# Transposing the first eight groups' input weights beside stage 0, and eight x tiles instead of ten

## The chip, the cores and the metric

The kernel runs on one NeuronCore of a Trainium2 chip. The metric is the device time of one execution in microseconds (us). PE is the tensor engine (PEld its weight loads), DVE the vector engine, ACT the scalar engine, POOL the GpSimd engine, SP the engine that here only issues transfers. SBUF is the on-chip memory, PSUM the accumulators that PE writes.

## The reference, cut to what matters

Two layers, each added to its input. B = 64 batches, C = 128 channels, L = 2048 steps.

```python
W = weights[condition]                       # [64, 128, 128], one of 16 matrices for each batch
x = x + einsum('bct,bcd->bdt', x, W)         # layer 0: a projection of the channels
K = 2 * einsum('hn,hnl->hl', Ct, exp(dtA * arange(L))).real     # 64 complex modes for each channel
y = irfft(rfft(x, 2L) * rfft(K, 2L))[..., :L] + x * D           # layer 1: causal convolution by channel
x = x + y * (arange(L) < length)             # masked by each batch's length
```

Everything is float32.

## The kernel before, in words

L is cut into two segments of 1024 steps (`SEGS`). The kernel has three parts.

**Stage 0** projects segment 0. For each of the 64 batches, `batch0(b)` calls `project`: eight matmuls (line 472) into a PSUM tile of the tag `y`, a copy back into the x tile on ACT or DVE (line 474), and a transfer of 0.5 MiB to a scratch array in DRAM (`scr`, line 477, issued by ACT). An x tile `xb` holds two batches, 1 MiB. `fetch` (line 442, issued by SP) loads it. `batch0(2n)` fetches tile `n + AHEAD`, with `AHEAD = 9` and ten tiles in the pool `big`, so that tile n + 10 needs the buffer of tile n. Beside the batches run the parameters of layer 1: first the setup on DVE and ACT, then, in the loop over `now` from 12 to 63, the tables `es` of 16 groups of channel pairs (steps `angles`, `sines`, `products`) and the first lags of the convolution kernel (`lags`, `keep_lags`, `store_lags`).

**The loop** `iteration(i)` goes over 64 pairs of segment and group: i = 0 to 31 are the 32 groups of four channels of segment 0, i = 32 to 63 those of segment 1. Iteration i prepares item i + 1 and finishes item i. On PE it holds: the transposes of the input weights of item i + 1 (`input_weights`, line 799, segment 0 alone, four transposes into a PSUM tile of the tag `tr`, copied by ACT at line 800 into `bt`), the transposes of x (`turn`, line 816, tag `tr`), the matmuls with the input weights (`inputs`, line 838), the direct part of the convolution (`inside`, line 883), the part from the states (`read`, line 891), and, in segment 0, the projection of segment 1 in pieces of 512 steps (`some`, line 467, tag `tr`): 12 pieces ahead of the loop, the other 116 in 28 iterations. The tag `tr` has two buffers. DVE does the recurrence (`scan`, line 853) and the masked result (line 913).

The input weights `bt` of a group are the same in both segments. In segment 0 they are transposed and stored to DRAM (`keep_weights`, line 805, 256 KiB, issued by SP); in segment 1 SP loads them back (line 792).

**The x tiles of the loop** come from the same pool `big`: `load(i + 3)` at line 778 for item i + 3 and, for the projection, `fetches` (line 442) of one `xb` tile in most iterations. SP takes its instructions strictly in order: in iteration i they are `load(i + 3)`, the fetch, four stores of item i - 1 (line 927), and the store of the weights of item i + 1. Each transfer that needs a buffer waits on SP until that buffer's last user is done.

**Semaphores of transfers.** The transfers issued by SP and ACT share eight completion semaphores, taken in turn in recorded order. A transfer is not issued until the one eight places ahead of it in that order has landed. ACT issues the `scr` stores, so ACT itself stands still in such a wait, with all that is queued behind it.

Of the kernel before, what the change touches and what calls it, by code (L numbers as in the profile page):

```python
# [42 lines left out]
F32 = mybir.dt.float32  # L46
# [6 lines left out]
P = 128  # L53
# [16 lines left out]
TP = 4  # L70
# [305 lines left out]
def cond_resid_ssm_kernel(  # L376
# [13 lines left out]
    nc = tc.nc  # L390
# [3 lines left out]
    N = a_imag.shape[1]  # L394
    NS = len(SEGS)
# [6 lines left out]
    GP = 8 // KK  # L402
# [3 lines left out]
    NE = Q + 1  # L406
# [6 lines left out]
    I8 = mybir.dt.uint8  # L413
    const = ctx.enter_context(tc.tile_pool(name="const", bufs=1))
    tab = ctx.enter_context(tc.tile_pool(name="tab", bufs=1))
    big = ctx.enter_context(tc.tile_pool(name="big", bufs=10))
    s0 = ctx.enter_context(tc.tile_pool(name="s0", bufs=4))
    dram = ctx.enter_context(tc.tile_pool(name="dram", bufs=1, space=DRAM))
    psp = ctx.enter_context(tc.tile_pool(name="psp", bufs=1, space=PSUM))

    scr = [dram.tile([P, C, HL], F32, tag=f"scr{s}", name=f"scr{s}") for s in range(NS)]
    kpad = dram.tile([C, KP], F32, tag="kpad", name="kpad")
    btd = dram.tile([NG, P, GP * 4 * N], F32, tag="btd", name="btd")
    carry = dram.tile([NP, P, 2, B], F32, tag="carry", name="carry")

    ci = const.tile([1, B], I32, tag="ci", name="ci")
    wres = const.tile([P, S, C], F32, tag="wres", name="wres")
    ident = const.tile([P, P], F32, tag="ident", name="ident")
# [3 lines left out]
    xbs, w1s = {}, {}  # L432
    BT = 2
    QB = SL // BK
    AHEAD = 9
    WAHEAD = 3

    def fetch(s, n):

        xbs[s, n] = big.tile([P, BT, SL], F32, tag="x", name=f"xb_{s}_{n}")  # L440
        src = x[n * BT : (n + 1) * BT, :, s * SL : (s + 1) * SL]
        nc.sync.dma_start(xbs[s, n], src.rearrange("b c t -> c b t"))
# [39 lines left out]
    def batch0(b, copy=nc.scalar.copy):  # L482
        if b % BT == 0 and b // BT + AHEAD < B // BT:
            fetch(0, b // BT + AHEAD)
        if b + WAHEAD < B:
            weigh(0, b + WAHEAD)
        project(0, b, 0, psp.tile([P, QB, BK], F32, tag="y", name=f"p0_0_{b}", bufs=2), QB, copy)

    V = nc.vector
    es = [tab.tile([P, TP, 2, NE], F32, tag=f"e{g}", name=f"e_{g}") for g in range(NT)]  # L490
# [4 lines left out]
    def exps(g):  # L495

        for i in range(TP):
            nc.scalar.activation(es[g][:, i, 0, :], steps, AF.Exp, scale=par_of(DRE, g, i))  # L498
# [11 lines left out]
    with tc.tile_pool(name="setup", bufs=1) as setup:  # L510
# [4 lines left out]
        par = _Parameters(nc, setup, psp, wk, ident, log_dt, c_in, log_a_real, a_imag)  # L515
        for n in range(AHEAD):
            fetch(0, n)
# [103 lines left out]
    def partial_angles(k):  # L621

        own = parts[:, :, 0:NL]
        by_l = some_l.unsqueeze(1).to_broadcast([P, NP, NL])

        def of(row, n):
            return gtab[:, row, :].unsqueeze(2).to_broadcast([P, NP, n])

        if k == 0:
            V.tensor_tensor(own, of(FHI, NL), by_l, ALU.mult)  # L630
        elif k == 1:
            V.tensor_scalar(whole, own, MAGIC, MAGIC, ALU.add, ALU.subtract)
        elif k == 2:
            V.tensor_tensor(own, own, whole, ALU.subtract)
        elif k == 3:
            V.tensor_tensor(whole, of(FLO, NL), by_l, ALU.mult)
        elif k == 4:
            V.tensor_tensor(own, own, whole, ALU.add)
        else:
            V.tensor_tensor(parts[:, :, 0:8], parts[:, :, 0:8], of(PHI, 8), ALU.add)  # L640
            V.tensor_tensor(parts[:, :, 24:25], parts[:, :, 24:25], of(PHI, 1), ALU.add)
            V.tensor_scalar(last, parts[:, :, 24:25], MAGIC, MAGIC, ALU.add, ALU.subtract)
            V.tensor_tensor(last, parts[:, :, 24:25], last, ALU.subtract)
# [48 lines left out]
    def store_lags(g):  # L692
# [3 lines left out]
        for c in range(2):  # L696
            r0 = g % 4 * 8 + c
            nc.gpsimd.dma_start(to[c], krow[r0 : r0 + 3 * 34 + 1 : 34, :])

    SPAN = 28  # L700
    pieces = [(s, b, q) for s in range(1, NS) for b in range(B) for q in range(QB)]
    FILL = 12
# [2 lines left out]
    def due(i):  # L705

        return min(len(pieces), FILL + (len(pieces) - FILL) * (i + 1) // SPAN)

# [7 lines left out]
    def fetches(n):  # L716

        nonlocal begun
        while begun < min(n + BT * QB, len(pieces)):
            fetch(pieces[begun][0], pieces[begun][1] // BT)  # L720
            begun += BT * QB
# [19 lines left out]
    for now in range(12, B):  # L741
        batch0(now, V.tensor_copy if now < 18 else nc.scalar.copy)
        if now < 20:

            by_row = d_in.rearrange("(d c h j) -> c d j h", j=8, c=2, d=2)
            with nc.allow_non_contiguous_dma(reason="128 gains, four times"):
                for i, r in ((i, r) for i in range(TP) for r in range(4) if (i * 4 + r) // 2 == now - 12):
                    nc.gpsimd.dma_start(dcol[i * NR + r : (i + 1) * NR : 4, :], by_row[r % 2, r // 2])
        if now == 21:
            V.tensor_scalar(dcol, dcol, 1.0, None, ALU.add)  # L750
        if now < FIRST:
            partial_angles(now - 12)
        if now < 18:
            exps(2 * now - 20)
            exps(2 * now - 19)
        for lag, step in STEPS.items():
            g, odd = divmod(now - FIRST - lag, 2)
            if not odd and 0 <= g < NT:
                step(g)
        if now == 60:  # L760
            fetches(FILL)
    assert not ts and not ks
# [5 lines left out]
    xs, us, ss, bts, tts, ys = {}, {}, {}, {}, {}, {}  # L768
# [3 lines left out]
    def seg(i):  # L772
        return divmod(i, NG)
# [11 lines left out]
        nc.gpsimd.dma_start(tts[i], bass.AP(row.tensor, row.offset, [[1, P], [KP, CG], [1, Q]]))  # L785

    def input_weights(i):

        s, g = seg(i)
        bts[i] = s1.tile([P, GP, 4, N], F32, tag="bt", name=f"bt_{i}")  # L790
        if s > 0:
            nc.sync.dma_start(bts[i].rearrange("p d k m -> p (d k m)"), btd[g])
            return
        pb = psp.tile([P, GP, 4, N], F32, tag="tr", name=f"pb_{i}", bufs=2)
        for d in range(GP):
            pair = g * GP + d
            for part in range(2):
                to = pb[:, d, part : 4 - part : 3 - 2 * part, :]
                nc.tensor.transpose(to, es[pair // TP][:, pair % TP, part, 1:NE], ident)  # L799
        nc.scalar.copy(bts[i], pb)  # L800

    def keep_weights(i):
        s, g = seg(i)
        if s == 0 and NS > 1:
            nc.sync.dma_start(btd[g], bts[i].rearrange("p d k m -> p (d k m)"))

    def at(s, d, f):
# [126 lines left out]
    def iteration(i):  # L934

        nxt = i + 1 < NI
        if i + 2 < NI and seg(i + 2)[0] > 0:
            input_weights(i + 2)
# [3 lines left out]
        if nxt:  # L942
            toeplitz(i + 1)
            if seg(i + 1)[0] == 0:
                input_weights(i + 1)
            states(i + 1)
# [13 lines left out]
        if nxt:  # L960
            inputs(i + 1, CG - 1)
            keep_weights(i + 1)
            scan(i + 1, 0, 2 if seg(i + 1)[0] == 0 else 1)
# [46 lines left out]
```

## Time and profile before

| what | value |
|---|---|
| median of 3 runs | 1116.4 us (1115.19 to 1116.72) |
| the profiled execution | 1110.19 us, span 1108.4 us |
| PE busy | 1054.6 us, 95% of the span |
| DVE, ACT, POOL busy | 821.4, 673.7, 222.6 us |
| granted PE clock, mean | 0.989 |
| moved by DMA | 313.31 MB |
| chain that ended last | PE 82%, DMA 12%, DVE 3%, ACT 2% |

The page cuts the span into 40 slices of 27.7 us; in its rows each digit is a busy share in tenths. The chain is followed back from the last instruction, at each step to what released it. The wait list gives who waited for whom, the total in us, the times and the longest. "DMA" as a row is the mean busy share of the 16 DMA engines.

### The profile page before, as it was taken

Reading aid. Unit: us, or ns where it says so; the run is one execution under the profiler, and the core shown is the slowest. Engines: PE = TensorE matmul, PEld = TensorE weight load, DVE = VectorE, ACT = ScalarE, POOL = GpSimd, SP = SyncE. Lnnn points to the kernel's source line nnn. Section 1 sums busy time; section 2 is a strip of 40 time slices with the busy share of each in tenths; the row PEclk is TensorE's granted clock in tenths of the full one; section 3 lists DMA queues with packets and bytes.
Section 4 is the critical chain, followed back from the end, with each engine's and each line's share of the span. In section 5 each row is a group of like instructions: output and inputs, shape, how many; then the busy total and the mean of one; then the engine's idle time right before and its main releaser. Section 6 shows DMA issues by size and latency. Waiting matters only on the chain.

```text
span 1108.4 us, 24477 instructions
## 1 busy us (share of the span) xinstructions
PE 1054.6 (95%) x8842; PEld 752.7 (68%) x8842; DVE 821.4 (74%) x2914; ACT 673.7 (61%) x1103; POOL 222.6 (20%) x386
## 2 busy tenths in 40 slices
PE   5678888999999999999999999999999999999996
PEld 2122223677777776776777778788888888888885
DVE  7587730667667766766766768888888888888886
ACT  3486665666666666667656666656665666566552
POOL 3152332021121112112121111212111111111120
PEclk9799999999999999999999999999999999999999
DMA  9999999999999999999999878688878887888754
GB/s 346 414 405 395 398 397 375 406 324 282 343 304 287 302 309 297 296 311 297 289 303 304 253 234 230 212 222 242 226 214 228 236 230 209 234 233 224 213 164 119
DMA packets 142731, 313.31 MB, mean 283 GB/s; under 512 B 12882, under 2 KB 13010, under 8 KB 142610
## 3 DMA queue, kind: packets, MB, share of 16 engines
q1 hardware_dynamic: 96528, 218.65, 62.6%
q10 hardware_dynamic: 35106, 67.64, 16.0%
q0 software_dynamic: 10976, 25.45, 8.7%
q8 instruction: 70, 1.15, 0.4%
q14 instruction: 51, 0.42, 0.1%
HBM read 164.76 MB, written 146.93 MB: 281 GB/s over the span
## 4 chain that ended last, share of the span: by engine, by line
PE 82%; DMA 12%; DVE 3%; ACT 2%; issue 1%; ACTq 0%; SPq 0%; DVEq 0%
PE y L891 20%; PE y L883 20%; PE v L838 19%; PE tr L816 10%; PE p L467 9%; DMA xb<-in_x_dram 6%; DMA scr<-xb 4%; PE p L472 2%; PE pb L799 2%; DMA x<-scr 1%; DVE s L853 1%; ACT xb L474 1%; DVE xb L474 0%; DVE x L913 0%; ACT e L498 0%
## 5 line engine op out<-in xcount | busy, mean ns | idle before, releaser
L853 DVE SCALAR_TENSOR_TENSOR s<-s,ptab 128x128 f32<-128x128 f32 x1792 | 535.9, 344 | 193.7 <-ACT s L843 193.7
L843 ACT ACTIVATE s<-v,ptab 64x512 f32<-64x512 f32 (+1 forms) x512 | 335.6, 655 | 51.3 <-PE v L838 35.1
L883 PEld LDWEIGHTS y<-tt,u 128*128 128x128 f32 x2048 | 263.5, 192 | 80.5 <-issue 67.0
L883 PE MATMUL y<-tt,u 128*128 128x128 f32 x2048 | 269.9, 275 | 0.1
L891 PEld LDWEIGHTS y<-e,s 64*128 64x128 f32 (+1 forms) x4096 | 219.0, 181 | 52.1 <-issue 26.6
L838 PE MATMUL v<-u,bt 128*128 128x512 f32 (+1 forms) x512 | 248.7, 567 | 0.3 <-ACT s L843 0.3
L817 ACT COPY u<-tr 128x512 f32<-128x512 f32 x252 | 148.1, 588 | 152.4 <-PE tr L816 125.7
L891 PE MATMUL y<-e,s 64*128 64x128 f32 (+1 forms) x4096 | 237.3, 276 | 1.4 <-DVE s L853 1.4
L474 ACT COPY xb<-p 128x512 f32<-128x512 f32 (+1 forms) x186 | 133.2, 717 | 80.8 <-PE p L467 54.1
L913 DVE COPY_PREDICATED x<-mask,y 128x1024 f32<-128x1024 uint8 x128 | 166.7, 1302 | 1.0 <-PE y L891 1.0
L472 PE MATMUL p<-xb,w 128*64 128x512 f32 x512 | 128.3, 639 | 37.2 <-issue 15.6
L816 PE MATMUL tr<-ident,x 128*128 128x128 f32 x1024 | 155.5, 274 | 1.7 <-DMA x<-scr 0.9
L816 PEld LDWEIGHTS tr<-ident,x 128*128 128x128 f32 x1024 | 121.1, 141 | 51.4 <-issue 44.9
L456 POOL COPY w<-wres 128x128 f32 x125 | 53.7, 430 | 426.7 <-PE p L467 315.6
L467 PE MATMUL p<-xb,w 128*128 128x512 f32 x256 | 129.6, 596 | 0.9 <-issue 0.6
L472 PEld LDWEIGHTS p<-xb,w 128*64 128x64 f32 x512 | 38.2, 144 | 112.1 <-issue 106.9
L838 PEld LDWEIGHTS v<-u,bt 128*128 128x128 f32 x512 | 79.5, 191 | 14.9 <-issue 13.4
L785 POOL DMA_DIRECT2D tt<-kpad x64 | 50.5, 789 | 194.7 <-DVE s L853 166.6
L863 DVE TENSOR_SCALAR s<-s 128x64 f32<-128x64 f32 x448 | 86.5, 193 | 0.0
L826 POOL DMA_DIRECT2D s<-carry x64 | 44.9, 706 | 127.1 <-PE y L891 118.4
L800 ACT COPY bt<-pb 128x512 f32<-128x512 f32 x32 | 18.7, 586 | 79.8 <-PE pb L799 75.6
L874 POOL DMA_DIRECT2D carry<-s x64 | 43.6, 722 | 100.9 <-DVE s L853 92.1
(194 smaller groups left out, 357.6 us busy)
## 6 DMA issues: line engine op xcount, KB each, us to landing
xb<-in_x_dram SPq DMA_DIRECT2D x64, 1024.0 KB, 9.5
scr<-xb ACTq DMA_DIRECT2D x128, 512.0 KB, 7.7
x<-scr SPq DMA_DIRECT2D x64, 1024.0 KB, 8.3
out_dram<-x SPq DMA_DIRECT2D x130, 256.0 KB, 3.7
out_dram<-x SPq DMA_DIRECT2D x62, 512.0 KB, 4.6
tt<-kpad POOLq DMA_DIRECT2D x64, 256.0 KB, 5.6
btd<-bt SPq DMA_DIRECT2D x32, 256.0 KB, 4.6
bt<-btd SPq DMA_DIRECT2D x32, 256.0 KB, 4.8
```

The lines of the kernel that those rows point to most:

```text
L467: nc.tensor.matmul(ps[:, k], w1s[s, b], own[:, cols[0]], start=True, stop=True)
L472: nc.tensor.matmul(ps[c, k], w1s[s, b][:, c], own[:, cols[h]], start=True, stop=True)
L474: copy(own[:, cols], ps.rearrange("p k t -> p (k t)"))
L816: nc.tensor.transpose(tr[:, k, :], xs[i][:, n, k * Q : (k + 1) * Q], ident)
L817: (nc.vector.tensor_copy if i == 0 else nc.scalar.copy)(u, tr)
L838: nc.tensor.matmul(v[:, 0:nv], w, us[i, n].rearrange("p k r -> p (k r)")[:, 0:nv], start=True, stop=True)
L843: nc.scalar.activation(own[:, 0:nv], v[lanes, 0:nv], AF.Copy, scale=amp)
L853: nc.vector.scalar_tensor_tensor(new, src, factor, own, ALU.mult, ALU.add)
L863: nc.vector.tensor_scalar(old[d][:, 2], old[d][:, 0], -1.0, None, ALU.mult)
L883: nc.tensor.matmul(y[:, k, :], u[:, k, :], tts[i][:, n, :], start=(k == 0), stop=False, skip_group_check=True)
L891: nc.tensor.matmul(ys[i, d][rows, c, k, :], ss[i][half[c], d, part, k, :, :].rearrange("p f b -> p (f b)")[:, rows], es[pair // TP][half[c ...
L913: nc.vector.copy_predicated(xs[i][:, 2 * d : 2 * d + 2, :].rearrange("r c (k t) -> r c k t", k=KK), keep_k.unsqueeze(1).to_broadcast([P, 2 ...
```

## The change

A tile `bres` of 8 groups' input weights (16 KiB of each partition) is added. In stage 0, at `now` = 37, 39, ..., 51, a new function transposes the weights of one of the groups 0 to 7 and DVE copies them into it. In the loop, the first eight groups of both segments use that tile; they are neither transposed there, nor stored, nor loaded back. The room comes from the pool `big`: eight tiles of 8 KiB instead of ten, and `AHEAD` is 7 instead of 9.

```diff
-    big = ctx.enter_context(tc.tile_pool(name="big", bufs=10))
+    big = ctx.enter_context(tc.tile_pool(name="big", bufs=8))
...
+    RG = 8
+    bres = const.tile([P, RG, GP, 4, N], F32, tag="bres", name="bres")
...
-    AHEAD = 9
+    AHEAD = 7
...
+    def weights_of(g, copy):
+
+        pb = psp.tile([P, GP, 4, N], F32, tag="tr", name=f"pb_{g}", bufs=2)
+        for d in range(GP):
+            pair = g * GP + d
+            for part in range(2):
+                to = pb[:, d, part : 4 - part : 3 - 2 * part, :]
+                nc.tensor.transpose(to, es[pair // TP][:, pair % TP, part, 1:NE], ident)
+        copy(bres[:, g] if g < RG else bts[g], pb)
...
+        g, even = divmod(now - 37, 2)
+        if not even and 0 <= g < RG:
+            weights_of(g, V.tensor_copy)
...
     def input_weights(i):
-
         s, g = seg(i)
+        if g < RG:
+            bts[i] = bres[:, g]
+            return
         bts[i] = s1.tile([P, GP, 4, N], F32, tag="bt", name=f"bt_{i}")
         if s > 0:
             nc.sync.dma_start(bts[i].rearrange("p d k m -> p (d k m)"), btd[g])
-            return
-        pb = psp.tile([P, GP, 4, N], F32, tag="tr", name=f"pb_{i}", bufs=2)
...
-        nc.scalar.copy(bts[i], pb)
+        else:
+            weights_of(g, nc.scalar.copy)
...
-        if s == 0 and NS > 1:
+        if s == 0 and g >= RG:
             nc.sync.dma_start(btd[g], bts[i].rearrange("p d k m -> p (d k m)"))
```

More of the change, by code (lines that the diff above doesn't have):

```diff
@@ L792, in input_weights @@
             nc.sync.dma_start(bts[i].rearrange("p d k m -> p (d k m)"), btd[g])
-            return
-        pb = psp.tile([P, GP, 4, N], F32, tag="tr", name=f"pb_{i}", bufs=2)
[L795 to L799, printed above, removed]
-        nc.scalar.copy(bts[i], pb)
+        else:
+            weights_of(g, nc.scalar.copy)
     def keep_weights(i):
         s, g = seg(i)
-        if s == 0 and NS > 1:
+        if s == 0 and g >= RG:
             nc.sync.dma_start(btd[g], bts[i].rearrange("p d k m -> p (d k m)"))
```

## The prediction

> **What bounds the kernel now.** I read the page's slices first, then the chain of waits in order of time, then two stretches of busy time, then the waits of SP's queue and ACT's timeline, last the landing times of single transfers. The slices:
>
> ```profile
> PE   5678888999999999999999999999999999999996
> DVE  7587730667667766766766768888888888888886
> DMA  9999999999999999999999878688878887888754
> ```
>
> The kernel has two limits in turn. In the first seven slices (stage 0) DMA is full and PE is not; from the eighth on PE is full. The busy time of four stretches says it in numbers (PE, PEld, DVE, ACT, POOL, then PE's clock, DMA share, GB/s):
>
> ```profile
> 54.60:78.60 24.00, 17.45 (x68) 5.13 (x65) 20.83 (x28) 21.02 (x55) 15.54 (x22) 0.93 1.04 407
> 80.90:162.50 81.60, 69.99 (x509) 23.17 (x500) 52.46 (x110) 51.55 (x77) 25.86 (x60) 0.98 1.03 396
> 315.00:656.00 341.00, 341.00 (x2735) 244.96 (x2732) 238.57 (x921) 217.47 (x358) 61.12 (x103) 1.00 0.93 293
> ```
>
> A share of 1.03 to 1.05 is the most this trace shows. From 54.6 to 78.6 DVE and ACT are nearly full as well; in segment 0 of the loop DMA, at 0.93, is close behind PE. The chain in segment 0, when no projection is left, with two starts of an iteration:
>
> ```profile
> 685.87 0.58 PE pb L799 x4
> 686.46 0.44 PE tr L816 x4
> ...
> 695.21 3.48 PE y L891 x64
> 698.69 0.59 PE tr L816 x4
> ```
>
> PE follows PE without a gap, so whatever leaves PE shortens the iteration. SP's queue, and ACT in front of a transfer:
>
> ```profile
> SPq L442 <- DMA scr<-xb: 144.0, 32, 7.2
> SPq L442 <- DMA out_dram<-x: 30.7, 21, 2.7
> 32.64 1.28 ACT L498 ACT_TABLE_LOAD   x1 [4.27 <-DMA scr<-xb]
> ```
>
> The first row: in stage 0 the fetches stand waiting for a store to land, that is, for a buffer. The third: ACT can be held by a transfer's semaphore, here for 4.27 us.
>
> **The change, part by part.** All sums are made against the profiled execution, 1110.19 us (span 1108.4 and 1.8 around it), and carried over to the median of 1116.4, which stands 6.2 higher.
>
> *Transposes leave the loop.* An iteration that starts with `pb` spends 0.58 + 0.44 us up to the end of the first `tr`, one without 0.59: 0.44 us saved a group (four matmuls of 0.11). Group 0's transposes run at 192.3, while PE waits for the first x tile (landed at 193.7): nothing saved. Groups 1 to 7: 7 x 0.44 = 3.05. At group 1 there is more:
>
> ```profile
> 201.67 0.89 PE y L883 x8
> 202.57 0.56 issue
> 203.12 1.10 PE p L467 x2
> ```
>
> The projection waits 0.56 for a `tr` buffer, and what ACT has just finished (202.44 to 203.02) is the copy of `bt`. With neither tile nor copy, the wait should go; what is late next is the recurrence's input on ACT, which is not on the chain there. Sum: -3.6 us (bounds -3.0 and -3.6). The eight ACT copies (0.59 each) and the eight stores and eight loads of 256 KiB cost nothing either way: ACT is 64% busy in the loop, and the chain holds neither.
>
> *Transposes enter stage 0.* 32 transposes and 8 DVE copies of 128x512 (0.69 us in the row of the same DVE copy of `u`) lie between 99 and 157 us, where PE is busy 70.0 of 81.6 us, DVE 52.5, and DMA is full. I cost them at nothing; DMA is the cover. Without it they would be 8 x (0.44 + 0.69) = 9 us. They share the two `tr` buffers with the lags, so PE's lags wait for ACT's copy of the lags before; the batches have no more than 0.3 us of that to fear each, under the same cover.
>
> *Two buffers fewer, in stage 0.* The loads may run two tiles (2.10 MB) less ahead: at 0.407 MB/us 5.2 us of transfer at most, and 0 if DMA never runs dry. Where it would: from 54.6 to 78.6 ACT issues the stores of batches 12 to 20, eight batches in 24.0 us, at the pace of DVE and ACT (20.8 and 21.0 busy). Eight batches need 8.39 MB in and out, 20.6 us at 407 GB/s; the other 3.4 us were filled with loads running ahead. With eight buffers that stock is gone before 54.6 (the fetch of tile n waits for the store of tile n - 8, not n - 10), so DMA stands idle about 3.4 us. The same bytes are left to do, after 79 us DMA is the limit again: stage 0 ends 3.4 us later (bounds 0 and +5.2). The steady part is not hurt: tiles wait about 34 us between landing and use, and lose 10 of that.
>
> *Two buffers fewer, in the loop.* The two programs' instruction lists show a new order of buffers: `x` of item i + 3 takes that of item i - 2, and the `xb` tiles rotate over three, so the fetch of `xb` tile t + 3 of segment 1 waits on SP for the second `scr` store of tile t. Queued behind it on SP are four stores of the output, the weights' store and the next x load; those have time (an x tile lands some 20 us later than now, and 15 us before PE's need, by adding the waits to the present landings). But the eight semaphores close a ring: for t = 11 to 28, 18 tiles, the second store of tile t must wait on ACT until the load of tile t + 2 has landed, and that load waits for the second store of tile t - 1. One turn, a store's landing and a load's, must fit in the time per tile: second stores of tiles 10 and 28 are issued at 325.7 and 614.0, 16.0 us a tile. If it does not fit, ACT stops, its copies of `u` with it, and PE stops. Before, these stores wait for transfers that SP issued long ago. The price, from landings between 315 and 656: stores 5.3 to 10.4 us, median 6.7; loads 8.6 to 11.7, median 9.6; in stage 0, where load follows store in just this way, loads 7.8 at least. From 5.3 + 7.8 = 13.1 (nothing lost) to 10.4 + 9.6 = 20.0 (4.0 x 18 = 72 us). The nearest rows are first halves, stored with no load issued beside them, 6.0 and 6.3 us, and the median load: 15.6 to 15.9, a tie with 16.0. With a scatter of some 0.8 us a tie loses perhaps 0.25 a tile, 4.5 us; PE, two buffers of `tr` ahead, absorbs the first 1.5. I take +3.0. A gain is excluded: PE's work sets the floor.
>
> The Trainium skill's page "DMA: Bandwidth & Descriptors" (section on the anatomy of one DMA) fits a transfer, on GpSimd's path, as 2.0 us and its bytes at 436 GB/s. As an estimate from that page, load and store would take 4.4 and 3.2 us, the ring 7.6, and this term would be nothing. The rows above, 9.6 and 6.7 us under load, contradict the fit here, so the rows are used.
>
> Sum: -3.6 + 3.4 + 3.0 = +2.8: 1119.2 us.
>
> **The rivals.**
>
> *Faster: both prices vanish, 1112.8 us.* The mechanism is DMA that drains sooner: with fewer loads queued, stores land earlier, ACT's holds go (4.0 us before the store of batch 11), the stores of stage 0 come in time and DMA never runs dry; the same quicker landings open the ring. Then only -3.6 is left. It decides from the point where at most 1.4 of the 3.4 us are idle and the ring takes under 15 us. For it: the landings of 6 us where little else is queued. Against it: DVE and ACT at 21 of 24 us have nothing to go faster with.
>
> *No change: stage 0 pays, the ring holds.* -3.6 + 3.4: 1116.2 us. It needs stores and loads below 15.5 us together; the tie above makes it nearly as likely as my forecast.
>
> *The ring binds: 1134 us.* The medians sum to 16.3 and the second halves alone, 10 us, to more. At 1 us a tile: 18 - 3.6 + 3.4 = +17.8. Against it: the 10 us belong to stores issued together with a load, and the ring itself forbids that.
>
> That the change does less than it says is not open: the lists of instructions show the first eight groups' transposes, stores and loads gone from the loop.
>
> **How the numbers follow.** Forecast 0.30, no change 0.26, faster 0.24, ring 0.18; 0.02 for others. What a measurement of this kernel can tell from no change is about 0.2%, 2.2 us. The forecast lies mostly above that, with 0.04 of its 0.30 below: slower is 0.26 + 0.18 + 0.02, and 0.02 of the no-change case that strays above it: 0.48. Same is 0.24 + 0.04 = 0.28, faster 0.24. The range runs from just under the faster case, 1112.3, to the ring at 1 us a tile, 1134; a ring at 2 us and more is left out.
>
> **What would show it.** In the chain after: `tr` of 0.59 right behind `y` in the first iterations, each 15.8 instead of 16.3 us, and no wait of 0.56 at group 1. In stage 0: a DMA share below 1.0 between 55 and 80 us, and the first x load of the loop issued at about 190 instead of 186.4. In the loop from 340 to 615: ACT or PE waiting for DMA `xb<-in_x_dram`, a few us in all if I am right, none in the no-change case, 18 or more if the ring binds. SP's waits at line 442 should be on `scr` in the loop as well. I would be wrong at the root if stage 0 ended as before or if iterations 1 to 7 were not shorter.

## The result and the profile after

The changed kernel takes 1118.97 us in the median (1115.28 to 1124.80), the kernel before 1115.39 in the runs beside it: a ratio of 1.0037, with an interval of 1.0022 to 1.0052, so 2.5 to 5.8 us slower. Forecast were 1119.2 us and +2.8.

The profile that came with it is the longest execution of the changed kernel (1124.80), and the profile before was the shortest of its own (1110.19); what they differ by, 14.6 us, is for the most part not the change. So both kernels were profiled once more: 1114.40 us before (span 1112.6) and 1117.69 after (span 1115.9), 3.3 us apart, near the medians. Sizes are taken from this second pair, and the first pair is named where it is used. One pair of profiles is a thin ground for a size, so where the other kernels show the same stretch, their numbers stand beside it.

The slices of the profile after, first pair:

```profile
PE   5678898799999999999999999999999999999996
DVE  7586660276776686677668658998888888888886
DMA  9999999968879989888888897777787887788754
```

The order of the limits is the old one: DMA first, then PE. PE is full from the ninth slice on instead of the eighth, and DMA's digit is 9 for eight slices and then falls to 6, where before it stayed at 9 for 22: in the loop's first third DMA has room now. The hole that matters in stage 0 is too shallow for digits of tenths. The busy time of two stretches after, first pair (PE, PEld, DVE, ACT, POOL, then PE's clock, DMA share, GB/s):

```profile
54.60:78.60 24.00, 15.98 (x70) 4.73 (x66) 20.51 (x28) 20.93 (x55) 15.16 (x22) 0.99 0.93 332
315.00:656.00 341.00, 340.56 (x2734) 243.42 (x2734) 236.11 (x913) 218.00 (x358) 65.14 (x105) 1.00 0.89 303
```

In the first, DMA has fallen from 1.04 to 0.93 while DVE and ACT do what they did before: this is the idle time that was forecast. The second pair has the same hole (before, then after):

```profile
54.60:78.60 24.00, 15.77 (x68) 4.70 (x64) 20.40 (x27) 20.21 (x55) 16.33 (x23) 1.00 1.04 402
54.60:78.60 24.00, 16.53 (x70) 5.00 (x68) 21.38 (x30) 21.39 (x56) 15.20 (x22) 0.98 0.93 328
```

A share of 0.93 instead of 1.04 for 24.0 us is some 2.5 us of DMA not used. Counted in bytes the hole is larger: 74 GB/s less for 24.0 us is 1.8 MB, or 4.4 us at the 402 GB/s of before, since the packets of that stretch also took longer for their bytes. The chain of the second profile after, with the first x load of the loop and the start of iteration 1:

```profile
192.88 10.62 DMA x<-scr
...
203.64 1.94 PE tr L828 x8
205.58 2.02 PE v L850 x2
...
207.62 0.68 ACT s L855
...
224.08 3.48 PE y L903 x64
227.56 0.59 PE tr L828 x4
228.15 0.95 PE y L895 x8
```

The load starts at 192.88; in the second profile before the same steps read

```profile
189.08 8.34 DMA x<-scr
...
199.62 0.89 PE v L838 x2
...
200.53 0.68 ACT s L843
```

so stage 0 ends 3.8 us later, and the load itself takes 2.3 longer. Behind `y` there is now `tr` at once and no `pb`. One more difference stands in these lines. The first two matmuls `v` take 2.02 us after and 0.89 before, at a granted PE clock of 0.51 (from 203.5 to 207.6) against 1.00 (from 197.4 to 201.0). So the first `s` begins 4.1 us after the tile's landing instead of 3.1. Where the time went, from the ends of the iterations (the end of DVE's last masked result of each) in the second pair:

| stretch | before | after | difference |
|---|---|---|---|
| up to the issue of the first x load | 189.1 | 192.9 | +3.8 |
| that load | 8.3 | 10.6 | +2.3 |
| from its landing to the end of iteration 0 | 26.7 | 26.8 | +0.1 |
| iterations 1 to 6 | 98.3 | 96.1 | -2.2 |
| iterations 7 to 25 | 310.7 | 310.7 | 0.0 |
| iterations 26 and 27 | 33.6 | 33.6 | +0.1 |
| iteration 32 | 13.0 | 11.9 | -1.1 |

The sum is +3.0; of the 3.3 us between the spans the rest lies behind the last iteration. Iteration 32 took 12.5 in the first profile before, and 11.9 in two kernels below that leave the loop's program as it was, so its 1.1 is not put down to the change. The 3.8 is one draw: the first x load is issued at 186.4 to 192.3 in the five profiles with ten tiles in all of stage 0, and at 192.9 to 198.6 in the four with eight, 4.9 us later in the middle values.

In the loop the fetches now wait for scratch stores, as forecast (SP's waits from 320 to 640, first profile after):

```profile
SPq L445 <- DMA scr<-xb: 72.0, 21, 7.8
```

In that stretch neither ACT nor PE waits for a load of the projection in either profile after. Iteration 26 is worth a look, because ACT stands there in front of a scratch store (ACT's timeline, first profile after):

```profile
652.12 0.37 ACTq L480 DMA_DIRECT2D scr<-xb  x1
652.52 0.59 ACT L829 COPY u<-tr 128x512 f32<-128x512 f32 x1 [2.23 <-DMA x<-scr]
```

### The profile page after: what moved, and what is told of

It is laid out like the page before. It is cut to its first block, busy times and chain, and to the rows that moved or that the text cites. A ratio compares the mean times of both kernels' runs of the same rounds, so it can differ in the third digit from the quotient of the medians.

```text
span 1123.0 us, 24449 instructions
## 1 busy us (share of the span) xinstructions
PE 1062.6 (95%) x8842; PEld 754.2 (67%) x8842; DVE 826.3 (74%) x2922; ACT 670.0 (60%) x1095; POOL 226.1 (20%) x386
## 3 DMA queue, kind: packets, MB, share of 16 engines
q10 hardware_dynamic: 35106, 67.64, 15.9%
## 4 chain that ended last, share of the span: by engine, by line
PE 86%; DMA 7%; DVE 2%; ACT 2%; issue 2%; ACTq 0%; POOLq 0%; SPq 0%; POOL 0%; DVEq 0%
PE y L903 20%; PE y L895 20%; PE v L850 18%; PE tr L828 10%; PE p L470 9%; PE p L475 6%; DMA xb<-in_x_dram 3%; DMA scr<-xb 3%; DMA x<-scr 1%; PE pb L710 1%; ACT xb L477 1%; DVE s L865 1%; PE pk L681 1%; ACT e L501 0%; DVE xb L477 0%
## 5 line engine op out<-in xcount | busy, mean ns | idle before, releaser
L895 PEld LDWEIGHTS y<-tt,u 128*128 128x128 f32 x2048 | 263.4, 192 | 80.9 <-issue 67.0
L850 PE MATMUL v<-u,bt 128*128 128x512 f32 (+1 forms) x384 | 186.4, 567 | 0.4 <-ACT u L829 0.4
L475 PE MATMUL p<-xb,w 128*64 128x512 f32 x512 | 132.1, 653 | 38.4 <-issue 16.6
L459 POOL COPY w<-wres 128x128 f32 x125 | 57.8, 462 | 439.6 <-PE p L470 317.8
L875 DVE TENSOR_SCALAR s<-s 128x64 f32<-128x64 f32 x448 | 91.1, 203 | 0.0
L850 PEld LDWEIGHTS v<-u,bt 128*128 128x128 f32 x384 | 59.6, 191 | 10.8 <-issue 9.6
L850 PE MATMUL v<-u,bres 128*128 128x512 f32 (+1 forms) x128 | 63.8, 581 | 0.2 <-ACT s L855 0.2
```

The lines of the kernel that those rows point to most:

```text
L475: nc.tensor.matmul(ps[c, k], w1s[s, b][:, c], own[:, cols[h]], start=True, stop=True)
L850: nc.tensor.matmul(v[:, 0:nv], w, us[i, n].rearrange("p k r -> p (k r)")[:, 0:nv], start=True, stop=True)
L875: nc.vector.tensor_scalar(old[d][:, 2], old[d][:, 0], -1.0, None, ALU.mult)
L895: nc.tensor.matmul(y[:, k, :], u[:, k, :], tts[i][:, n, :], start=(k == 0), stop=False, skip_group_check=True)
```

## The experiments

In the diffs `...` marks lines left out. **Theory A** is the prediction's sum. **Theory B**, formed on the first profile after, holds that the loop pays nothing and stage 0 all. **Theory D** came after the first four runs: stage 0 pays for the missing tiles, and the loop's start pays because ACT's sixth scratch store waits for an x load.

### Fewer tiles alone

```diff
-    big = ctx.enter_context(tc.tile_pool(name="big", bufs=10))
+    big = ctx.enter_context(tc.tile_pool(name="big", bufs=8))
...
-    AHEAD = 9
+    AHEAD = 7
```

> The kernel before with eight x tiles and a lead of seven tiles, and nothing else: the weights are transposed, stored and loaded in the loop as before. Theory A (the prediction): two tiles fewer cost 3.4 us in stage 0 and 3.0 us in the loop, so the kernel before plus 6.4 us (ratio 1.006), and the changed kernel is 3.6 us faster than this one. Theory B (after the changed kernel's trace): the ring of stores and loads costs nothing in the loop, all the cost lies ahead of the loop: plus 6 to 7 us, the first x load of the loop issued 5 us or more later than 186.4, and iterations of 16.26 us throughout. Theory C (the transposes in stage 0 are not hidden and are what costs): this kernel stands within 1 us of the kernel before.

Measured: 1124.50 us against 1115.22 before, ratio 1.0106 (1.0076 to 1.0135). Theory C, named in this expectation, is out: the tiles cost, and more than 6.4 us. The hole from 54.6 to 78.6 is there (0.96, 339 GB/s), and the first x load is issued at 193.8. Iteration 0 ends 29.1 us after that load has landed, not 26.7, with a granted PE clock of 0.50 in the first 4.1 us. Some of the cost lies in the loop, against theory B: iterations 6, 7 and 26 are 0.3, 0.9 and 2.9 us longer than before, and iterations 1 to 27 together 3.3 us, since iterations 8 and 27 give 0.5 us back each. In iteration 7 it is the very wait that the prediction feared, ACT in front of a scratch store for a load of the projection (the chain of this kernel):

```profile
331.58 6.61 DMA xb<-in_x_dram
```

The chain holds it once, not in 18 tiles; in iteration 26 it is an x load, 6.61 us as well. So eight tiles did cost 3 us in the loop while the weights were still stored and loaded there, and hardly any in the changed kernel. Why is not shown; the stores and loads left out change which transfer each semaphore waits for.

### Ten tiles and no transposes in the loop

```diff
-    big = ctx.enter_context(tc.tile_pool(name="big", bufs=8))
+    big = ctx.enter_context(tc.tile_pool(name="big", bufs=10))
...
-    AHEAD = 7
+    AHEAD = 9
...
-        copy(bres[:, g] if g < RG else bts[g], pb)
+        copy(away if g < RG else bts[g], pb)
...
-            bts[i] = bres[:, g]
+            bts[i] = wres[:, 0 : 2 * GP, :].rearrange("p (d a) (b m) -> p d (a b) m", d=GP, b=2)
```

(`away` is one small tile that takes the place of `bres`. This kernel and the next multiply the first eight groups with the table `wres`, so they leave out those groups' weights and serve for times alone.)

> The changed kernel with ten x tiles and a lead of nine, as before. The room for the eight groups' weights is not there, so the transposes of stage 0 are copied over one another into one small tile, and the loop multiplies the first eight groups with a constant table instead of their weights; the instructions, sizes and engines are those of the changed kernel. Theory A and B: only the gain is left, the kernel before minus 2.6 to 3.6 us (ratio 0.997), the first x load of the loop issued at 186 to 187, iterations 0 to 6 of 15.9 us. Theory C (transposes in stage 0 not hidden, up to 9 us): slower than before by 1 to 6 us.

Measured: 1117.40 us, ratio 1.0020 (0.9998 to 1.0041). This fits none of A and B: the gain alone should be left, and it is gone. Theory C, 1 to 6 us slower, would fit the time; the kernel with the transposes alone, below, excludes it. The loop did gain (iterations 1 to 6 are 15.9 us), and DMA was full from 54.6 to 78.6 (1.04, 407 GB/s). The loss is in iteration 0, which ends 32.1 us after the first x tile has landed instead of 26.7. ACT's timeline there:

```profile
195.83 0.58 ACT L476 COPY xb<-p 128x512 f32<-128x512 f32 x1 [0.27 <-PE p L469]
205.83 0.37 ACTq L479 DMA_DIRECT2D scr<-xb  x1
206.48 2.78 ACT L855 ACTIVATE s<-v,ptab 64x512 f32<-64x512 f32 x4 [10.06 <-DMA x<-scr]
```

ACT finishes a copy at 196.4, stands until 205.8 in front of the store of that copy, and the recurrence's inputs `s` are queued behind. It waits for an x load: the eight semaphores are taken in turn, and without the store of group 0's weights the load of x tile 3 moves ahead of the sixth scratch store in that order, takes the semaphore of x tile 0's load, and leaves the store the one that the load of x tile 1 holds. Before, the store got that of x tile 0, which lands earlier (193.7), and was issued at 193.8. The changed kernel has the same stop (second profile after, from 196.0 to 206.3):

```profile
195.38 0.58 ACT L477 COPY xb<-p 128x512 f32<-128x512 f32 x1 [0.27 <-PE p L470]
206.28 0.37 ACTq L480 DMA_DIRECT2D scr<-xb  x1
207.62 5.57 ACT L855 ACTIVATE s<-v,ptab 64x512 f32<-64x512 f32 x8 [11.66 <-PE v L850]
```

### The same with one store put back

```diff
-        if s == 0 and g >= RG:
+        if s == 0 and (g >= RG or g == 0):
             nc.sync.dma_start(btd[g], bts[i].rearrange("p d k m -> p (d k m)"))
```

> The kernel with ten x tiles and a constant table as the first eight groups' weights, with one transfer put back: the store of group 0's weights to DRAM at the loop's start (256 KiB). It takes a semaphore of its own, and the sixth scratch store of the loop's start no longer gets the one that the load of x tile 1 holds. Theory D: ACT's wait of 10 us before that store goes, iteration 0 ends 26 to 27 us after the first x tile has landed instead of 32.1, and the kernel is 4 to 5 us faster than without that store: the kernel before minus 2 to 3 us. Rival (the transposes in stage 0 cost 5 us): no change against the kernel without the store, the kernel before plus 2 us.

Measured: 1111.85 us against 1116.39, ratio 0.9963 (0.9947 to 0.9979), the one kernel that is faster than before, by 4.5 us where 2 to 3 were expected. The two intervals against before do not touch: 0.9998 to 1.0041 without the store, 0.9947 to 0.9979 with it. ACT's timeline shows the stop gone, the store following its copy at once:

```profile
197.09 0.58 ACT L476 COPY xb<-p 128x512 f32<-128x512 f32 x1 [0.27 <-PE p L469]
197.71 0.37 ACTq L479 DMA_DIRECT2D scr<-xb  x1
203.79 1.38 ACT L855 ACTIVATE s<-v,ptab 64x512 f32<-64x512 f32 x2 [6.12 <-PE v L850]
```

Iteration 0 ends 27.9 us after the landing, not 32.1 (26 to 27 were expected; the granted clock was 0.50 in the first 4.1 us). So a store of 256 KiB more makes the kernel some 6 us shorter (from 1.0020 to 0.9963); iteration 0 accounts for 4.2 of them, the rest is not traced. Theory D holds here in the cause, and the rival, transposes in stage 0 that cost 5 us, is out.

### The transposes in stage 0 alone

```diff
+    bts = {}
...
     def weights_of(g, copy):
...
+        copy(away if g not in bts else bts[g], pb)
```

(In stage 0 as in the changed kernel, with `away` as the target; the loop is that of before.)

> The kernel before with the stage-0 transposes of groups 0 to 7 added (32 transposes, 8 copies on DVE into one small tile that nothing reads); ten x tiles, the loop as before with its own transposes. Theory A (hidden under DMA, as predicted): the kernel before within 1 us. Rival (they slow the batches or the transfers: the kernel with ten tiles and no transposes in the loop was 2.2 us slower, not 2.7 faster): plus 4 to 5 us, with the last store of segment 0 landing at 190 or later in place of 186.2. Theory D (that kernel lost its 5 us at the loop's start, where ACT stood 10 us in front of the sixth scratch store for the load of x tile 1): the kernel before within 1 us, and ACT's sixth scratch store issued without such a wait.

Measured: 1115.54 us against 1116.39, ratio 0.9996 (0.9980 to 1.0012). The 32 transposes and 8 copies cost nothing there that is clear of the noise, at most 1.3 us by the interval, and the last store of segment 0 lands at 188.3, not at 190 or later. That DMA is what hides them fits, by its share of 1.03 from 80.9 to 162.5.

### The changed kernel with the store put back

The edit is that of the third experiment, in the changed kernel.

> The changed kernel with the same one store put back, of group 0's weights from the resident tile. Theory D: ACT no longer stands 10 us in front of the sixth scratch store; here x tile 0 lands late as well, so only part of it was on the chain: 1 to 3 us faster than the changed kernel, the kernel before plus 1 to 3 us. Rival: the same as the changed kernel, plus 4 us.

Measured: 1119.28 us against 1116.39, ratio 1.0029 (1.0011 to 1.0047). The stop in front of the sixth store is gone (it follows its copy at 198.35), but the time is the changed kernel's within the intervals. Of the 1 to 3 us expected nothing is clear of the noise; the rival holds. With eight tiles the first x tile lands late as well, and from its landing to the end of iteration 0 pass 27.0 us here and 26.8 to 27.7 in the two profiles of the changed kernel, so there was almost nothing to win. The step costs 4 to 6 us in one kernel and next to none in the other.

### Four groups, nine tiles

```diff
-    big = ctx.enter_context(tc.tile_pool(name="big", bufs=8))
+    big = ctx.enter_context(tc.tile_pool(name="big", bufs=9))
...
-    RG = 8
+    RG = 4
...
-    AHEAD = 7
+    AHEAD = 8
```

> The changed kernel for four groups instead of eight: weights of groups 0 to 3 kept (8 KiB of each partition), nine x tiles, a lead of eight. The gain is 3 x 0.37 to 0.44 and 0.6 at group 1, 1.7 to 1.9 us. Theory A and B: one tile's stock instead of two is missing from 54.6 to 78.6, 1.05 MB or at most 2.6 us, of which the kernel needs 3.4 us less what nine tiles still hold: 0.8 to 1.7 us lost; in all within 1 us of the kernel before. Rival (a cost that is there as soon as one tile is missing, as a changed order of buffers would make it): plus 2 us or more.

Measured: 1121.68 us, ratio 1.0069 (1.0047 to 1.0091). A miss for A and B; the rival, 2 us or more, holds. It is not even faster than with eight groups (the intervals just overlap). Two things are seen. The hole from 54.6 to 78.6 is there with nine tiles as with eight:

```profile
54.60:78.60 24.00, 18.73 (x76) 5.64 (x72) 20.65 (x26) 19.07 (x53) 15.86 (x24) 0.94 0.91 326
```

One missing tile is enough here, so the loss does not go by the bytes of the missing tiles. And ACT stands before the sixth store from 199.6 to 209.1, for the same semaphore, and iteration 0 ends 28.8 us after the landing. Against that only four groups gain.

### Giving up the two tiles later

```diff
+        if b in (30, 38):
+            both = big.tile([P, BT, SL], F32, tag="x", name=f"bres_{k}")
...
+        ahead = AHEAD - (b >= 30) - (b >= 38)
```

> The changed kernel with ten x tiles at first: the room for the weights of groups 0 to 3 is taken from the x tiles at batch 30 and that of groups 4 to 7 at batch 38, so the loads run nine tiles ahead up to there, then eight, then seven. The loop is that of the changed kernel, with eight tiles. Theory A (DMA idles for want of stock from 54.6 to 78.6 us): that idle time goes, 3.4 us, and the ring's 3.0 us stay: the kernel before minus 0.6 us. Theory B (no price in the loop): minus 2 to 3 us, ratio 0.9975, DMA share of 1.03 and more from 54.6 to 78.6. Rival (eight tiles cost in all of stage 0, at its end and at the loop's start as well): no better than the changed kernel by more than 1 us, plus 2 to 4 us.

Measured: 1128.99 us, ratio 1.0129 (1.0101 to 1.0158). DMA was indeed full from 54.6 to 78.6 (1.03), but something else came up (waits from 100 to 185):

```profile
DVE bres L721 <- DMA scr<-xb: 11.9, 2, 7.4
...
PEld pk L691 <- DVE bres L721: 10.8, 2, 6.7
```

The tile seems to get its place only when it is first written, and by then the free place was that of an x tile just projected: no run shows the rule itself, but the wait went when the place was held. DVE's copy of the weights stood for that tile's store, and PE for DVE. So each place was held from the batch that takes it:

```diff
+            nc.sync.dma_start(both[:, 0, 0:4], weights[0, :, 0:4])
```

(in the place of the fetch that is left out, and with the store of group 0's weights put back.)

> The changed kernel, with ten x tiles at first and the two tiles for the weights taken at batches 30 and 38, each held from there on by a transfer of 2 KiB that SP issues into it in the place of the fetch left out, and with the store of group 0's weights put back at the loop's start. Theory D: DMA is not idle from 54.6 to 78.6 us (the changed kernel lost some 3.5 us there), DVE never waits for a scratch store (two waits of 7.4 and 4.5 us in the kernel that took the tiles late without holding them), ACT does not stand in front of the sixth scratch store; left are the gain of iterations 0 to 6, 2.2 us, and the hold at iteration 26, 0.9 us: the kernel before minus 1 to 4 us. Rival (fewer tiles slow the load packets themselves, whenever it is that they are fewer): plus 1 to 3 us.

Measured: 1119.44 us against 1117.70, ratio 1.0018 (0.9993 to 1.0042): the 1 to 4 us are not gained, and the rival's 1 to 3 fits without being clear of the noise. DVE's waits are gone, but the hole has moved. Its busy time, in the old stretch and from 110 to 140, where the tiles have been taken away:

```profile
54.60:78.60 24.00, 15.31 (x61) 4.57 (x58) 19.85 (x26) 18.55 (x52) 15.90 (x21) 0.90 1.03 381
110.00:140.00 30.00, 27.88 (x208) 9.73 (x204) 21.00 (x45) 18.68 (x29) 11.04 (x25) 1.00 0.94 329
```

The second profile before has 1.04 there, the second after 1.03. The load of tile 24 is issued at 118.1, against 107.4 and 112.3 in the two profiles before. What the rival names is seen too: the load packets took longer once the tiles were fewer (the numbers are in the last section).

### Twelve groups, seven tiles

```diff
-    big = ctx.enter_context(tc.tile_pool(name="big", bufs=8))
+    big = ctx.enter_context(tc.tile_pool(name="big", bufs=7))
...
-    RG = 8
+    RG = 12
...
-    AHEAD = 7
+    AHEAD = 6
```

> The changed kernel for twelve groups, seven x tiles, a lead of six: in the loop the tiles of the projection have two buffers instead of three, so the load of tile t + 2 waits for the second store of tile t, and tile t + 2 is needed one tile's time (16 us) after that store is issued. In the changed kernel that store took 3.2 to 6.2 us and the load 6.3 to 9.3. Theory D: store and load, 10 to 16 us, still fit; the loop gains 10 x 0.37 us = 3.7, DMA in stage 0 is idle for 5 to 8 us for want of three tiles' stock, ACT stands 10 us before the sixth scratch store again (it would get the semaphore of x tile 1): the kernel before plus 5 to 9 us. Rival (the ring of the prediction binds at two tiles): 1 us and more lost in each of 20 iterations, plus 20 us or more.

Measured: 1194.64 us against 1117.70, ratio 1.0718 (1.0673 to 1.0763), 77 us slower in the medians. Theory D is out, and the rival's 20 us and more holds: iterations 8 to 27 are 77 us longer together. But the ring is another one than drawn. ACT's and PE's waits between 320 and 640:

```profile
ACT bt L711 <- DMA btd<-bt: 67.4, 9, 9.2
...
PE p L470 <- ACT bt L711: 39.2, 9, 6.2
```

and the chain through one turn:

```profile
443.94 3.20 DMA scr<-xb
...
450.75 8.04 DMA btd<-bt
...
458.87 0.59 ACT bt L711
```

The fetch stands on SP for the scratch store. Behind it, in SP's order, stand the four stores of the output and the weights' store. ACT's next copy of `bt` needs the buffer which that store reads, PE needs the `tr` buffer which that copy frees, and the next scratch store comes late. The loads themselves were in time: from tile 14 of segment 1 on, a tile had landed 14 to 24 us before its first scratch store was issued.

### Both kernels once more

> The kernel before, unchanged, for a second profile. The first profile (1110.19 us) is the shortest of its executions, 5 us under the median. If what varies between executions is the time of the load packets in stage 0 (the first profile: 2.6 us per DMA engine above 159 ns a packet; the changed kernel: 11.1), a second profile near the median shows 6 to 9 us there, a last store of segment 0 at about 191, and iterations of 16.26 and 12.25 us as before.

Measured: 1114.40 us. The last store of segment 0 landed at 188.9, not 191, and the load packets took 5.1 us per DMA engine above 159 ns: below the 6 to 9 expected. The iterations are as before.

> The changed kernel, unchanged, for a second profile: its first one (1124.8 us) is the longest of its executions, 6 us above the median. Theory D: DMA idle in stage 0 again 3 to 4 us more than before, iterations 1 to 6 of 15.9 us, ACT's hold of 10 us before the sixth scratch store and a hold of about 1 us in iteration 26 again; the time of load packets above 159 ns lower than 11.1 us per DMA engine, and the whole time near 1119. Rival (the long load packets come with the change): 10 us or more of them again.

Measured: 1117.69 us. The hole (some 2.5 us, where 3 to 4 were expected), the stop before the sixth store and iterations of 15.9 us are all there again; iteration 26 is 0.6 us longer than before. The load packets take 6.6 us instead of 11.1.

## Why the prediction was right, and where its steps were not

**The bound.** Right: DMA in stage 0, PE in the loop, in every profile but that of twelve groups.

**Transposes leave the loop, -3.6.** The mechanism is right, and the size was nearly so: -2.2 in iterations 1 to 6, and some 0.9 in iteration 0 that the total does not show. Iterations 1 to 6 end 0.37 us sooner each (15.89 instead of 16.26). The first `y` behind the first `tr` now takes 0.95 where it took 0.89, which eats 0.07 of the 0.44. At group 1 the wait of 0.56 is gone from the chain, and from the first `s` on iteration 0 takes 22.7 us (second profile after) instead of 23.6. But that first `s` begins 4.1 us after the landing instead of 3.1, because PE was granted half its clock until then, and so iteration 0 ends 26.8 us after the landing, as before. The kernels of twelve groups and of tiles given up later and held, with the same loop here, repeat it: `s` after 4.0 and 3.7 us, then 22.7 and 22.8. (In the first profile after it is 23.5, with a granted clock still at 0.78 from 4.1 to 8 us behind the landing.) In both profiles before the clock was 1.00 there. That the clock takes the gain back is worked out from these profiles; no run holds the clock at 1.00 with the transposes gone. The text looked at ACT's recurrence input as what is late next; it had no term for the clock of PE.

**Transposes enter stage 0, 0.** Right within the noise, by the kernel with them alone (0.9996, 0.9980 to 1.0012).

**Two buffers fewer, in stage 0, +3.4.** Right in place, with some 2.5 us of DMA idle from 54.6 to 78.6, and near in size: +3.8 between the second profiles, +4.9 between the middle values of all profiles with ten and with eight tiles, +12.3 between the first pair. The reasoning by bytes of stock is not borne out: nine tiles have the same hole as eight. And giving up the tiles later moved the hole instead of closing it. That the missing tiles make the hole is shown: four profiles with eight tiles and the one with nine have it (0.91 to 0.96, 321 to 339 GB/s), seven with ten tiles up to there do not (1.03 to 1.04, 381 to 407 GB/s); the one with seven lies between (0.99, 349 GB/s).

**Two buffers fewer, in the loop, +3.0.** Wrong. Iterations 7 to 25 cost nothing. The mis-sized terms are store and load: second stores took 4.2 us and loads 7.5 (medians from 325 to 625, first profile after), 11.7 together, where the nearest rows had given 15.6 to 15.9, and less than the 13.1 of its favourable end. The load's 9.6 came from a loop with second stores of 8.9 us (median; the text said 10) beside it. The ring parts the two: the text said so of the stores, and did not carry it into the loads. The estimate from the Trainium skill's page "DMA: Bandwidth & Descriptors" (anatomy of one DMA) was 7.6 us for the two; the measured 11.7 lies between it and the rows used, and below the 16.0 that the loop gives. ACT's waits on transfers exist, but singly: 0.1 to 0.9 us net in iterations 26 and 27, and the 10 us before the sixth store, of which the late x tile left nothing on the chain.

**What the sum did not hold.** Two terms at the loop's start. The first x load takes 10.6 instead of 8.3 us, +2.3. It goes with the scratch stores still out when it is issued: with four out it took 10.3 to 10.6 us (both profiles after, and twelve groups), with two or three 7.4 to 8.7 (the ten other profiles). That the stores are the cause, and why four are out, no run shows. And PE runs at a granted clock of 0.51 from the landing until the first `s`, +1.0. In each of the eleven profiles besides the two before, PE had a clock of 0.50 for some part of the first 8 us after the landing. It had stood idle for 7.4 and 8.3 us ahead of it in the changed kernel, for 0.9 and 2.4 before; but with idle times of 2.3 to 2.8 us it was halved in four other kernels, so which idle time brings it on is open.

So the forecast of +2.8 and the measured +3.6 in the medians agree by luck, because errors cancel: 3.0 paid in the loop that were not due, against 2.3 for the first load and 1.0 for the clock at the loop's start that were forgotten, with half a us too much gained and, by the second pair, 0.4 too little charged to stage 0. Of the cases, the loop behaved as in the no-change rival (stage 0 pays, the ring holds), and the time came out as in the forecast. The faster rival is refuted by the hole. A ring does bind one tile further down, though through the weights' store and not the one that the text drew.

**The version that gains.** Ten tiles and the weights kept would give about 0.9963 by the kernel that stands for it, which has a constant table in place of the weights; there is no room for both. Of those that compute the whole, none was shown to beat the kernel before.

## What to carry to other kernels

When buffers are traded for saved work, price the trade in each stage: here PE's saving of some 3 us was real, and the stage bound by DMA paid 3.8 or more for the tiles. Look at the granted clock behind each long wait too: 4 us at half clock took back 1 us of that saving. When transfers share a few completion semaphores in turn, taking one transfer out changes whom all later ones wait for; list, for each store that a computing engine issues, which transfer it now waits for, before and after. When a ring of transfers seems to tie with the time it has, take its terms from rows in which the transfers run as alone as the ring will make them.

## What was not expected of the hardware

The load packets of stage 0 (4096 bytes, mostly 159 ns) have a tail: in the second profile before, 190 of the 7976 from 20 us on took over 300 ns, and single packets took up to 2.0 us. Summed over 159 ns and divided by the 16 DMA engines this is time in which DMA counts as busy and moves less. Between the two profiles before it is 2.6 and 5.1 us, and stage 0 ends at 186.4 and 189.1; between the two after it is 11.1 and 6.6, and stage 0 ends at 198.6 and 192.9. The loops of each pair agree to 0.1 us in nearly every iteration, so most of what the two profiles of each kernel differ by lies in stage 0, and most of that is of this size. Kernels with ten tiles throughout show 2.6 to 6.7 us (five profiles), with eight 6.6 to 11.1 (four), with nine 8.2 and with seven 6.0. The tail goes with the stretch in which tiles are missing. From 20 to 110 us it is 1.2 to 3.7 us in the seven profiles that have ten tiles there, and 4.2 to 5.8 in the six that have fewer. From 110 on it is 6.8 and 7.0 us in the two kernels that give up tiles then, and 1.4 to 5.6 in the others. So fewer tiles and longer packets come together; which of the two brings the other about, or what brings both, stays open.
